# Spectral filter products in column halves, with the moving operand read in memory order

## Chip, cores and metric

The kernel runs on one core of one Trainium2 chip. The metric is device microseconds (us) of the whole program, median of three runs. A core has five engines that run side by side, each through its own list of instructions in order: TensorE (PE in the profile; its weight loads are a row of their own, PEld), VectorE (DVE), ScalarE (ACT), GpSimd (POOL) and SyncE (SP), which here issues all DMAs. Engines wait for each other through semaphores. Matmul results land in PSUM, from where VectorE or ScalarE copy them to SBUF.

## What is computed

Two layers, each with a convolution block done in the frequency domain and a small quantised feed-forward block, on x of shape 8 x 128 x 128 x 96. What matters here is the filter of the convolution block. For each of three scales a coarse complex filter `cw` (rows h, columns w, 192 channels, real and imaginary part) is resized with two cubic matrices, one over rows and one over columns, to 128 x 65 frequencies:

```python
SCALE_HW = [(16, 9), (8, 4), (24, 13)]
x_pre = _soa(jnp.einsum('bhwc,mc->bhwm', x, w1), soa1_scale, soa1_bias)
xf = jnp.fft.rfft2(x_pre.transpose(0, 3, 1, 2), axes=(2, 3), norm='ortho').transpose(0, 2, 3, 1)
for cw in (cw0, cw1, cw2):
    Rh = _resize_mat(cw.shape[0], FH)
    Rw = _resize_mat(cw.shape[1], FWH)
    t = jnp.einsum('Hh,hwmc->Hwmc', Rh, cw)
    t = jnp.einsum('Ww,Hwmc->HWmc', Rw, t)
comb = jnp.einsum('shwm,bsm->bhwm', filt, r.astype(filt.dtype))
xff = xf * comb
```

`r` is a softmax per image over the three scales. The resize over w does not depend on the image, so it is done once for each layer; the one over h, with the image's `r` in it, is done for every image.

## The kernel before

**Stages.** Each image of each layer (16 jobs) is cut into 16 groups. Stage P (`pixels`) normalises 8 rows of pixels, multiplies by w1, and does the first Fourier transform; it ends in DRAM (`a_d`). Stage F (`frequencies`) takes 4 of the 65 columns of frequencies at a time: it loads P's result (`al`) and the filter rows (`ut`), multiplies `ut` by the image's gate on GpSimd (L712), resizes over h on TensorE (`pf`, L724), transforms (`py`), multiplies, and transforms back (`pz`, `pi`). Stage S (`tokens`) ends the inverse transform and does the feed-forward block.

**Order.** The stages run beside each other, one group of each per iteration. The order of all engines' work in an iteration is written out by hand in lists of (stage, step, how many groups ahead): RAMP while only P runs (t from -5 to 14), RISE while P and F run (t from 15 to 34), TICK for the long steady state, then FALL and TAIL. Every engine gets its instructions in this order.

**The filters.** "U" entries in RAMP and RISE are `filters` (L288 to L316), a generator of four steps: the matmuls over w, the ScalarE copies, the VectorE copies, the store to DRAM (`u_d`, read again as `ut` by every F group). A unit covers 8 of the 96 rows (48 coarse rows, real and imaginary) for all 192 channels. There are 12 units for each layer: layer 0's are in RAMP at t = 3 to 14, layer 1's in RISE at t = 21 to 32. The filter is kept as `cw`, 26 partitions (the coarse columns of the three scales) in each of four bands of 32 partitions, one band for 48 channels, with [channel, row] along the partition. A unit is four matmuls, 26 rows deep, 65 columns of weights (`k_rw`), and 384 moving columns (8 rows x 48 channels), one from each band. Their moving operand is read with rows outermost, so neighbouring elements are 96 words apart:

```python
pss[i].rearrange("p (n m) -> p n m", m=UM),
kt["rw"][32 * i : 32 * i + NWS],
cws[l][32 * i : 32 * i + NWS, :, n0 : n0 + UN].rearrange("p m n -> p n m"),
```

The four products lie in four PSUM banks: two of the pair `ps_u` (tag d0) and `ps_v0`, `ps_v1` (tags s3, s4). Two ScalarE copies (L308) and two VectorE copies (L310) of 65 x 384 take them to SBUF, and one DMA (L315) stores 65 x 8 x 192.

**PSUM tags.** A tile waits until the last reader of the tile before it with the same tag is done. In RAMP, d0 is shared by `pa0` (the first transform's product, read by L621 and L622) and `ps_u`; d1 by `pa1` and `pt_a`; d2 by `pw0` and `pw1`; s3 by `ps_v0` and the set-up matmuls' `ps_w`.

**A ramp iteration.** TensorE: U, `pt_a` (L567), `pw` (L578), `pa` twice (L605), `pw`. VectorE: two `at` (L621, L622) of the group before, statistics `st` (L492), the U copies, two `sd` (L596), the norm's small ones ending in `n_rs` (L526), one `sd` (L596), two `at`. GpSimd: two `acc` (L590), `xn_a` (L563, as soon as `n_rs` is there), one `sd`. The `sd` tiles have two buffers, so the last VectorE `sd` of an iteration also waits until the first `pa` has read the older one.

**Set-up.** `background` (L430 to L451) holds the loading of filters and weights in small portions. The main loop takes one portion each iteration, after step 9 of stage P (L1056 to L1058), from t = 0 on. Layer 0's four `cw` loads (L286) are one portion, at t = 0.

Of the kernel before, what the change touches and what calls it, by code (L numbers as in the profile page):

```python
# [11 lines left out]
F32 = mybir.dt.float32  # L12
# [9 lines left out]
M = 2 * C  # L22
# [15 lines left out]
NKC = NKW // KC  # L38
PACK = NKC // 2
GK = 68  # L40
UM = 48
UN = 8
NU = NG // UN
NA, NY = 3, 3
LAG = 3
UAHEAD, UPAUSE, UEND = 3, 18, 35
# [72 lines left out]


RAMP_BANKS = {
    "pa0": 0, "pa1": 1, "pw0": 2, "pw1": 2, "pt_a": 1, "ps_u": 0, "ps_v0": 3, "ps_v1": 4,
}
BANKS = {
    "ps_g": 4, "ph": 3, "pl": 4, "pa0": 1, "pa1": 0, "pw0": 0, "pw1": 0, "pt_a": 0,
# [4 lines left out]
RISE_BANKS = {  # L130
    "ps_g": 3, "ph": 3, "pl": 3, "pa0": 2, "pa1": 0, "pw0": 0, "pw1": 2, "pt_a": 2,
    "pf0": 0, "pf1": 2, "py0": 1, "py1": 1, "pz0": 3, "pz1": 4, "pi0": 3, "pi1": 4,
    "px": 3, "pg": 3, "ps_u": 0, "ps_v0": 3, "ps_v1": 4,
}
FALL_BANKS = {
    "pf0": 0, "pf1": 2, "py0": 1, "py1": 1, "pz0": 3, "pz1": 4, "pi0": 3, "pi1": 4,
# [32 lines left out]
def _constants():  # L169

    n = np.arange(128)
    ang = 2 * np.pi * ((n[:, None] * n[None, :]) % 128) / 128
    cos, sin = np.cos(ang), np.sin(ang)

    even, odd = np.arange(0, 65, 2), np.arange(1, 64, 2)
    bins = ((1, even), (-1, even[1:-1]), (1, odd), (-1, odd))


    f_w = np.concatenate([cos[:64, b] if c > 0 else -sin[:64, b] for c, b in bins], 1) / 128
    f_w = np.concatenate([f_w, f_w], 0)  # L180


    fwd, inv = [], []
    for p in range(2):
        c, s = cos[:HH, p::2], sin[:HH, p::2]
        fwd.append(np.block([[c, -s], [s, c]]))
        inv.append(np.block([[c.T, s.T], [-s.T, c.T]]))

    fwd0, inv0 = np.zeros((2, HH, 2, 2, 2, HH // 2)), np.zeros((2, 2, HH // 2, 2, 2, HH))
    for p in range(2):  # L190
        c, s = cos[:HH, p:HH:2].copy(), -sin[:HH, p:HH:2]
        two = np.full((1, HH // 2), 2.0)
        if p == 0:
            s[:, 0] = cos[:HH, HH]
            two[0, 0] = 1.0
        for b in range(2):
            fwd0[b, :, p, 0, b], fwd0[b, :, p, 1, b] = c, s
            inv0[0, b, :, p, b], inv0[1, b, :, p, b] = (c * two).T, (s * two).T
    fwd0, inv0 = fwd0.reshape(128, 2, 128), inv0.reshape(128, 2, 128)

    d = np.concatenate([cos[b] if c > 0 else -sin[b] for c, b in bins], 0) * 2 / 128
    d[0] /= 2
    d[32] /= 2
    d = d[:, :HH]
    rh = np.concatenate([_resize_mat(h, H) for h, _ in SCALES], 1).T
    rh0 = np.zeros((GP, 2, 2, HH // 2))
    for p in range(2):
        f = np.arange(p, HH, 2)
        rh0[:NHS, 0, p] = (rh[:, f] + rh[:, -f % 128]) / 2
        rh0[64:, 1, p] = (rh[:, f] - rh[:, -f % 128]) / 2  # L210
    rh0[:NHS, 1, 0, 0] = rh[:, HH]
    rh = np.concatenate([rh[:, 0::2], rh[:, 1::2]], 1)
    rh2 = np.zeros((GP, 128))
    rh2[:NHS] = rh
    rh2[64:] = rh
    rw = np.concatenate([_resize_mat(w, NKW) for _, w in SCALES], 1).T
    rw = np.concatenate([rw[:, odd], rw[:, even]], 1)
    rw4 = np.zeros((128, NKW))
    for i in range(M // UM):
        rw4[32 * i : 32 * i + NWS] = rw  # L220
    made = dict(
        dft=f_w, fwd=np.stack(fwd, 1), inv=np.stack(inv, 1), idft=d, rh=rh2, rw=rw4,
        fwd0=fwd0, inv0=inv0, rh0=rh0.reshape(GP, 128),
    )
    return {k: np.ascontiguousarray(v, dtype=np.float32) for k, v in made.items()}
# [15 lines left out]
def metaformer_kernel(ctx: ExitStack, tc: tile.TileContext, x, cst, layers, out):  # L241
# [30 lines left out]
    nc.vector.memset(ones, 1.0)  # L272

    mid = [dram.tile([W, H, C], F32, name=f"mid{b}") for b in range(B)]
    u_d = [dram.tile([NKW, GP, M], F32, name=f"u_d{l}") for l in range(len(layers))]
    a_d = [dram.tile([128, HH, 2, M], F32, name=f"a_d{i}") for i in range(NA)]
    y_d = [dram.tile([128, HH, 2, C], F32, name=f"y_d{i}") for i in range(NY)]


    def load_filters(l, p):  # L280

        cws[l] = us.tile([128, UM, NG], F32, name="cw")
        for i in range(M // UM):
            if l and i:
                yield
            nc.sync.dma_start(cws[l][32 * i : 32 * i + NWS], p["cw"][:, i * UM : (i + 1) * UM, :])  # L286

    def filters(i):  # L288

        l, n0 = i // NU, i % NU * UN  # L290
        pu = bank2("ps_u")
        pss = [pu[:NKW, i, : UN * UM] for i in range(2)]
        pss += [bank1(f"ps_v{i}")[:NKW, : UN * UM] for i in range(2)]
        for i in range(M // UM):
            mm(
                pss[i].rearrange("p (n m) -> p n m", m=UM),
                kt["rw"][32 * i : 32 * i + NWS],
                cws[l][32 * i : 32 * i + NWS, :, n0 : n0 + UN].rearrange("p m n -> p n m"),
                start=True,
                stop=True,  # L300
            )
        yield
        u = us.tile([NKW, UN, M], F32, name="u", bufs=3)
        uv = u.rearrange("p n (i m) -> p i n m", m=UM)
        for i, ps in enumerate(pss):
            o = ps.rearrange("p (n m) -> p n m", m=UM)
            if i < 2:
                nc.scalar.copy(uv[:, i], o)  # L308
            else:
                nc.vector.tensor_copy(uv[:, i], o)  # L310
            if i == 1:
                yield
        yield
        n1 = n0 if n0 < NHS else 64 + n0 - NHS
        nc.sync.dma_start(u_d[l][:, n1 : n1 + UN, :], u)  # L315
        yield  # L316

    def padding(l):
# [110 lines left out]

    def background():  # L430

        yield from load_filters(0, layers[0])
        constants("rw")
        yield
        yield from other_weights(0, layers[0])
        for k in ("fwd", "rh"), ("inv", "rh0"), ("fwd0", "inv0"), ("idft",):
            constants(*k)
            yield
        padding(0)
        yield  # L440
        cw1 = load_filters(1, layers[1])
        for k, _ in enumerate(token_weights(0, layers[0])):
            if k >= 3:
                next(cw1)
            yield
        for _ in cw1:
            yield
        yield
        yield from projection_weights(1, layers[1])
        for _ in zip_longest(other_weights(1, layers[1]), token_weights(1, layers[1])):  # L450
            yield  # L451
# [244 lines left out]
    def frequencies(jb, k):  # L696
# [7 lines left out]
        for p, first in enumerate((re, im)):  # L704
            for e in range(2):
                nc.sync.dma_start(al[64 * p : 64 * p + 64, e], av[:, e, first : first + KC])
        ud = u_d[jb.l].rearrange("k n m -> n k m")
        nc.sync.dma_start(ut[:, 1:], ud[:, k0 : k0 + KC])
        if packed:
            nc.sync.dma_start(ut[:, :1], ud[:, NKW - 1 :])  # L710
# [304 lines left out]
    with tc.manual_schedule():  # L1015
        advance("P", 0, 0)
        start = projection_weights(0, layers[0])
        for _ in range(4):
            next(start)
        events = background()  # L1020
        for t in range(-first, n + offset["S"] + behind + 1):
            norms.append(Norms())
            if t < offset["F"] - 4:
                order, places, late_steps = RAMP, RAMP_BANKS, {}
            elif t < offset["S"] - 2:
                order, places, late_steps = RISE, RISE_BANKS, RISE_GATE
                on_pool.update(sd=())
            elif t < n + 2:
                order, places, late_steps = TICK, BANKS, GATE
            elif t <= n + offset["F"]:  # L1030
                order, places, late_steps = FALL, FALL_BANKS, {}
            else:
                order, places, late_steps = TAIL, TAIL_BANKS, {}
                on_act.update(norm=NORM_ACT_TAIL, cast=CAST_ACT_TAIL, out=False)
            banks.update(places)
            if t == UEND:
                padding(1)
                early.close()
                pools.append(ctx.enter_context(tc.tile_pool(name="sb", bufs=2)))
            gates = {}  # L1040
            for late, into in late_steps.items():
                if (t - late) % NRG == NRG - 1 and 0 <= t - late < n:
                    for place, step in into:
                        gates.setdefault(place, []).append((step, (t - late) // NRG))
            for place, (stage, step, ahead) in enumerate(order):
                for gate_step, image in gates.get(place, ()):
                    advance("G", gate_step, image)
                i = t - offset[stage] + ahead
                last = i if stage == "N" else group(i) if stage == "U" else min(i, n - 1)
                advance(stage, step, last)  # L1050
                if (stage, step, i) == ("N", 0, 1):
                    for late in 1, 2:
                        advance("N", late, i)
                    for _ in start:
                        pass
                if (stage, step) == EVENTS_AFTER:  # L1056
                    if t >= 0:
                        next(events, None)  # L1058


# [38 lines left out]
```

## Time and profile before

| | us |
|---|---|
| median of 3 runs (4893.21 to 4893.49) | 4893.36 |
| the profiled execution's own time | 4890.47 |
| its span in the trace | 4888.7 |

The trace's mean TensorE clock is 0.989 of full. The page gives busy times of engines, a strip of 40 slices of the span, the chain of work that ended last (followed back from the end, at each step to what released it), and the costliest groups of instructions with the mean duration of one. The trace behind the page also answers for a stretch of time: instructions in order, waits, busy times. Times in it are us from the start of the span; a row with "x8" is eight instructions merged. A float32 matmul shows as two records. The ramp runs to 137 us, the fill (first frequencies of the first image) from there to about 174 us, RISE to about 440 us.

### The profile page before, as it was taken

How to read it: one execution, taken by the hardware profiler on the slowest of the kernel's cores; microseconds unless marked ns; L12 is line 12 of the kernel's file. 1: busy time of each engine (PE TensorE's matmuls, PEld its weight loads, DVE VectorE, ACT ScalarE, POOL GpSimd, SP SyncE). 2: the span in 40 equal slices, each digit the busy share in tenths (PEclk: the TensorE clock that was granted, in tenths of full speed). 3: DMA queues.
4: the chain of work that ended last, by engine and by line, in shares of the span. 5: the costliest groups of instructions: out<-in, count | busy, mean ns of one | idle time of the engine just before them, and what ended most of it. 6: DMA issues, size and time to landing. Idle time of an engine off the chain costs nothing.

```text
span 4888.7 us, 123746 instructions
## 1 busy us (share of the span) xinstructions
PE 4799.7 (98%) x44232; PEld 3744.3 (77%) x44232; DVE 4593.7 (94%) x13942; ACT 4311.6 (88%) x7103; POOL 2530.5 (52%) x1884
## 2 busy tenths in 40 slices
PE   8999999999999999999999999999999999999997
PEld 5677777777777777777777778777777777777764
DVE  8888999999999999999999999999999999998998
ACT  7556999999999999999999999999999999998887
POOL 4444555555555555555555555555555555554544
PEclk9999999999999999999999999999999999999996
DMA  6767777777777777777777777777777777777754
GB/s 203 203 192 202 213 213 217 214 213 214 214 214 213 215 214 214 215 212 221 212 214 217 209 216 214 216 215 214 213 214 215 215 214 213 215 215 196 208 168 125
DMA packets 917424, 1020.96 MB, mean 209 GB/s; under 512 B 75826, under 2 KB 848914, under 8 KB 916602
## 3 DMA queue, kind: packets, MB, share of 16 engines
q1 hardware_dynamic: 916810, 1013.04, 74.7%
q8 instruction: 353, 5.78, 0.5%
q14 instruction: 261, 2.14, 0.1%
HBM read 598.92 MB, written 413.84 MB: 207 GB/s over the span
## 4 chain that ended last, share of the span: by engine, by line
PE 90%; DVE 5%; ACT 3%; issue 1%; SPq 0%; POOL 0%; DMA 0%; POOLq 0%; DVEq 0%; ACTq 0%
PE pw L578 17%; PE py L758 14%; PE pz L848 9%; PE pa L605 7%; PE pf L724 7%; PE pi L864 7%; PE pm L943 6%; PE pz L840 5%; PE po L960 5%; PE pt_a L567 5%; PE ps_r L898 4%; PE pt_c L933 2%; DVE st L492 1%; ACT y L946 1%; DVE xr L909 1%
## 5 line engine op out<-in xcount | busy, mean ns | idle before, releaser
L801 POOL TENSOR_TENSOR xf<-pr 128x768 f32<-128x768 f32 x512 | 931.2, 1819 | 416.4 <-DVE pr L786 391.3
L578 PE MATMUL pw<-w,xT 97*128 97x240 f32 x4096 | 942.6, 373 | 6.4 <-DVE at L622 2.9
L758 PE MATMUL py<-k_fwd,al 128*128 128x128 f32 (+1 forms) x6208 | 799.2, 280 | 0.0
L946 ACT CAST y<-pm 128x1024 f16<-128x1024 f32 x768 | 754.8, 1017 | 42.8 <-PE pm L943 42.6
L578 PEld LDWEIGHTS pw<-w,xT 97*128 97x128 f32 x4096 | 741.6, 191 | 59.7 <-ACT r L581 10.9
L953 ACT ACTIVATE h<-a 128x1024 fp8e5<-128x1024 f16 x731 | 775.4, 1061 | 0.2 <-DVE a L949 0.2
L590 POOL TENSOR_TENSOR acc<-acc,r 128x192 f32<-128x192 f32 x496 | 295.8, 596 | 924.1 <-ACT r L581 859.0
L758 PEld LDWEIGHTS py<-k_fwd,al 128*128 128x128 f32 (+1 forms) x6208 | 741.9, 190 | 40.9 <-DVE pr L786 3.3
L978 POOL TENSOR_TENSOR y<-xr,o 128x768 f32<-128x768 f32 x256 | 422.0, 1648 | 677.1 <-DVE o L975 600.9
L581 ACT ACTIVATE r<-pw 128x960 f32<-128x960 f32 x512 | 496.9, 970 | 127.0 <-PE pw L578 125.9
L782 DVE TENSOR_TENSOR pr<-py,cf 128x768 f32<-128x768 f32 x512 | 486.4, 950 | 49.7 <-PE py L758 36.4
L596 DVE TENSOR_TENSOR sd<-xs 128x384 f32<-128x384 f32 x1008 | 521.2, 557 | 1.5 <-ACT xs L584 0.8
L712 POOL TENSOR_TENSOR ut<-ut,rw 112x768 f32<-112x768 f32 (+1 forms) x256 | 473.2, 1848 | 39.0 <-DMA ut<-u_d 34.0
L724 PEld LDWEIGHTS pf<-k_rh,ut 48*128 48x128 f32 x6080 | 360.4, 188 | 151.7 <-issue 140.8
L943 PE MATMUL pm<-xq,f_q 96*128 96x512 fp8e5 x1536 | 431.3, 390 | 27.9 <-ACT y L946 22.0
L563 POOL TENSOR_TENSOR xn_a<-xt,n_rs 128x768 f32<-128x768 f32 x256 | 381.5, 1490 | 128.2 <-DVE n_rs L526 113.1
L936 ACT ACTIVATE xq<-pt_c 96x1024 fp8e5<-96x1024 f32 x256 | 260.8, 1019 | 201.7 <-PE pt_c L933 201.7
L584 ACT ACTIVATE xs<-r 128x768 f32<-128x768 f32 x512 | 436.6, 853 | 0.4
L724 PE MATMUL pf<-k_rh,ut 48*128 48x128 f32 x6080 | 410.1, 281 | 7.5 <-POOL ut L712 3.5
L919 ACT ACTIVATE xn_c<-xr,n_nb,n_rs 128x96 fp8e5<-128x96 f32 x1056 | 412.5, 489 | 0.0
L864 PE MATMUL pi<-zt,k_inv 128*128 128x384 f32 (+1 forms) x1024 | 394.1, 505 | 2.3 <-ACT zt L855 2.2
L848 PE MATMUL pz<-w2c,xf 128*128 128x96 f32 x2048 | 396.0, 275 | 0.0
(133 smaller groups left out, 10124.3 us busy)
## 6 DMA issues: line engine op xcount, KB each, us to landing
a_d<-at SPq DMA_DIRECT2D x256, 768.0 KB
al<-a_d SPq DMA_DIRECT2D x1024, 192.0 KB
y_d<-yt SPq DMA_DIRECT2D x512, 192.0 KB
v<-y_d SPq DMA_DIRECT2D x256, 384.0 KB
ut<-u_d SPq DMA_DIRECT2D x256, 336.0 KB
xt<-in_x_dram SPq DMA_DIRECT2D x512, 96.0 KB
xr<-in_x_dram SPq DMA_DIRECT2D x256, 192.0 KB
mid<-y SPq DMA_DIRECT2D x256, 192.0 KB
```

Source lines behind the costliest of these rows:

```text
L578: mm(o, xT[:, 4 * a + 2 * i + j, :], wt["w1"], start=True, stop=True)
L581: nc.scalar.activation(r.rearrange("p a s c -> p a (s c)"), pw, AF.Relu)
L596: on.tensor_tensor(sd[:, e], xs[:, 0], xs[:, 1], op)
L724: mm(pf[:, i, t * 128 : (t + 1) * 128], utf[64 * i : 64 * i + NHS, c0 : c0 + 128], kt["rh"][64 * i : 64 * i + NHS, :], start=True, stop=True,)
L758: mm(py[p0:p1, t, e, :], alf[:, e, c0 + p0 : c0 + p1], f, start=True, stop=True)
L782: nc.vector.tensor_tensor(p0, yv, crb, ALU.mult)
L801: nc.gpsimd.tensor_tensor(xf.rearrange("p t e f -> p (t e) f"), pr[:, 0].rearrange("p t r k -> p t (r k)"), pr[:, 1].rearrange("p t r k -> ...
L848: mm(pz[t][:, j, e, :], xf[:, 2 * t, e, :], wt["w2c" if t else "w2a"], start=False, stop=j == e == 1,)
L864: mm(pi[e][:, lo : KC * C], kt["inv"][:, e, :], zt[:, e, lo:], start=True, stop=True)
L943: mm(pm[:, s, :], fk, xq[:, s, :], start=True, stop=True)
L946: nc.scalar.copy(y16, pm)
L953: nc.scalar.activation(hk, a16, AF.Copy, saturate=False)
```

## The change

Filter products have 64 columns of weights instead of 65; `cw` lies in two bands of 32 partitions with 96 channels each; a unit covers 4 coarse rows of the real and the same 4 of the imaginary part. The four matmuls of a unit are two bands times two halves of the PSUM partitions (0 to 63 real, 64 to 127 imaginary). The moving operand is read in memory order, 4 neighbouring rows of a channel, then the next channel. One ScalarE and one VectorE copy of 128 x 384, reading PSUM with a step of 4 elements, turn it to [row, channel]. Two DMAs store a unit. The 65th frequency, whose weights only pick the last column of each scale, comes from six small loads, two transposes, one ScalarE copy and two stores for each layer. `ps_u` is gone. Portions of `background` are smaller and more, and begin at t = -3. The rows of `u_d` are padded from 112 to 128.

```diff
-UM = 48
-UN = 8
-NU = NG // UN
+UN = 4
+HC = C // 2
+NU = NHS // UN
...
-    "pa0": 0, "pa1": 1, "pw0": 2, "pw1": 2, "pt_a": 1, "ps_u": 0, "ps_v0": 3, "ps_v1": 4,
+    "pa0": 0, "pa1": 1, "pw0": 2, "pw1": 2, "pt_a": 1, "ps_v0": 3, "ps_v1": 4,
...
-    rw4 = np.zeros((128, NKW))
-    for i in range(M // UM):
-        rw4[32 * i : 32 * i + NWS] = rw
+    rw2 = np.zeros((64, 64))
+    for h in range(2):
+        rw2[32 * h : 32 * h + NWS] = rw[:, :-1]
...
-    u_d = [dram.tile([NKW, GP, M], F32, name=f"u_d{l}") for l in range(len(layers))]
+    u_d = [dram.tile([NKW, 128, M], F32, name=f"u_d{l}") for l in range(len(layers))]
...
     def load_filters(l, p):
 
-        cws[l] = us.tile([128, UM, NG], F32, name="cw")
-        for i in range(M // UM):
-            if l and i:
+        cws[l] = us.tile([64, C, NG], F32, name="cw")
+        for h in range(2):
+            for n in range(0, C, HC):
+                nc.sync.dma_start(
+                    cws[l][32 * h : 32 * h + NWS, n : n + HC],
+                    p["cw"][:, C * h + n : C * h + n + HC, :],
+                )
                 yield
-            nc.sync.dma_start(cws[l][32 * i : 32 * i + NWS], p["cw"][:, i * UM : (i + 1) * UM, :])
+        last = us.tile([C, 2, NG], F32, name="cw_last")
+        h0 = w0 = 0
+        for h, w in SCALES:
+            w0 += w
+            to = last.rearrange("p u (r n) -> p u r n", r=2)[:, :, :, h0 : h0 + h]
+            end = p["cw"][w0 - 1].rearrange("(u p) (r n) -> p u r n", u=2, r=2)
+            for u in range(2):
+                nc.sync.dma_start(to[:, u], end[:, u, :, h0 : h0 + h])
+            h0 += h
+        yield
+        ps = bank1("ps_w")[:NG, :M]
+        for u in range(2):
+            nc.tensor.transpose(ps[:, u * C : (u + 1) * C], last[:, u], ident[:C, :C])
+        ends = us.tile([NG, M], F32, name="cw_end")
+        nc.scalar.copy(ends, ps)
+        yield
+        for r in range(2):
+            nc.sync.dma_start(u_d[l][NKW - 1, 64 * r : 64 * r + NHS, :], ends[NHS * r : NHS * r + NHS])
 
     def filters(i):
 
         l, n0 = i // NU, i % NU * UN
-        pu = bank2("ps_u")
-        pss = [pu[:NKW, i, : UN * UM] for i in range(2)]
-        pss += [bank1(f"ps_v{i}")[:NKW, : UN * UM] for i in range(2)]
-        for i in range(M // UM):
-            mm(
-                pss[i].rearrange("p (n m) -> p n m", m=UM),
-                kt["rw"][32 * i : 32 * i + NWS],
-                cws[l][32 * i : 32 * i + NWS, :, n0 : n0 + UN].rearrange("p m n -> p n m"),
-                start=True,
-                stop=True,
+        pss = [bank1(f"ps_v{h}")[:, : UN * C] for h in range(2)]
+        for h, ps in enumerate(pss):
+            q = slice(32 * h, 32 * h + NWS)
+            for i in range(2):
+                n1 = NHS * i + n0
+                mm(
+                    ps[64 * i : 64 * i + 64].rearrange("p (m n) -> p m n", m=C),
+                    kt["rw"][q],
+                    cws[l][q, :, n1 : n1 + UN],
+                    start=True,
+                    stop=True,
+                )
+        yield
+        u = us.tile([128, UN, 2, C], F32, name="u", bufs=3)
+        nc.scalar.copy(u[:, :, 0], pss[0].rearrange("p (m n) -> p n m", m=C))
+        yield
+        nc.vector.tensor_copy(u[:, :, 1], pss[1].rearrange("p (m n) -> p n m", m=C))
+        yield
+        for i in range(2):
+            nc.sync.dma_start(
+                u_d[l][:64, 64 * i + n0 : 64 * i + n0 + UN, :].rearrange("k n m -> k (n m)"),
+                u[64 * i : 64 * i + 64].rearrange("p n h m -> p (n h m)"),
             )
...
     def background():
 
+        constants("rw")
         yield from load_filters(0, layers[0])
-        constants("rw")
-        yield
         yield from other_weights(0, layers[0])
...
         for k, _ in enumerate(token_weights(0, layers[0])):
-            if k >= 3:
+            if k >= 1:
                 next(cw1)
             yield
-        for _ in cw1:
-            yield
-        yield
+        yield from cw1
...
-        ud = u_d[jb.l].rearrange("k n m -> n k m")
+        ud = u_d[jb.l].rearrange("k n m -> n k m")[:GP]
...
                 if (stage, step) == EVENTS_AFTER:
-                    if t >= 0:
+                    if t >= -3:
                         next(events, None)
```

## Prediction, made before the changed kernel was run

> **What bounds the kernel now.** I read the page's totals first, then the answer for the filter's tile, then the chain of waits in the ramp and in RISE, then the instructions in order of time where VectorE and GpSimd meet. Totals:
>
> ```profile
> span 4888.7 us, 123746 instructions
> PE 4799.7 (98%) x44232; PEld 3744.3 (77%) x44232; DVE 4593.7 (94%) x13942; ACT 4311.6 (88%) x7103; POOL 2530.5 (52%) x1884
> PE 90%; DVE 5%; ACT 3%; issue 1%; SPq 0%; POOL 0%; DMA 0%; POOLq 0%; DVEq 0%; ACTq 0%
> ```
>
> TensorE carries the whole, but VectorE is close behind, and the change only touches the ramp and RISE (the steady state's lists of instructions stay as they are). The answer for the tile ps_u:
>
> ```profile
> L295 PE MATMUL ps_u<-cw,k_rw x96: 804/816/836, 48.0 to 387.3; 26*65 26x384 f32 x96
> L308 ACT COPY u<-ps_u x48: 474/476/478, 49.6 to 388.5; 65x384 f32<-65x384 f32 x48
> ```
>
> A record of a filter product takes 816 ns (the middle figure). The first transform pa (L605), also 384 columns, takes 482 ns a record in the same stretch: the stepped read costs about twice. What a unit costs on the path is in the chain (start, us, what), here one ramp iteration:
>
> ```profile
> 100.22 0.77 PE ps_u L295 x2
> 100.99 0.01 PE ps_v L295 x2
> 101.00 0.63 PE ps_u L295 x2
> 101.63 0.01 PE ps_v L295 x2
> 101.65 1.01 PE pt_a L567 x8
> 102.65 1.62 PE pw L578 x8
> 104.28 1.45 PE pa L605 x16
> 105.73 1.82 PE pw L578 x8
> 107.55 0.77 PE ps_u L295 x2
> ```
>
> The iteration is 107.55 - 100.22 = 7.33 us, TensorE without a gap; the unit is 0.77 + 0.01 + 0.63 + 0.01, with starts 1.43 apart. Four products run at once (the ps_v rows add 0.01). In RISE the chain shows the same 1.43 (272.91 to 274.34) within iterations of about 16 us, again all TensorE. So the unit lies on the path in all 24 of its places.
>
> One thing could spoil this. In the ramp VectorE is busy 76.92 of 81.5 us (48.03 to 129.53). Its last sd of an iteration behaves in two ways. First an iteration before the units begin, then one with them:
>
> ```profile
> 37.48 0.17 DVE L526 SCALAR_TENSOR_TENSOR n_rs<-n_a,n_rs 128x8 f32<-128x8 f32 x1
> 37.73 1.47 POOL L563 TENSOR_TENSOR xn_a<-xt,n_rs 128x768 f32<-128x768 f32 x1 [2.21 <-DVE n_rs L526]
> 37.74 1.88 DVE L596 TENSOR_TENSOR sd<-xs 128x384 f32<-128x384 f32 x1
> ```
>
> ```profile
> 97.72 0.17 DVE L526 SCALAR_TENSOR_TENSOR n_rs<-n_a,n_rs 128x8 f32<-128x8 f32 x1
> 97.89 0.56 DVE L596 TENSOR_TENSOR sd<-xs 128x384 f32<-128x384 f32 x1
> 97.96 1.82 POOL L563 TENSOR_TENSOR xn_a<-xt,n_rs 128x768 f32<-128x768 f32 x1 [3.27 <-DVE n_rs L526]
> ```
>
> Whichever of sd and xn_a starts first runs through; if it is xn_a, sd takes 1.88 instead of 0.56, and in those iterations TensorE's pt_a stands 1.56 us for L622 (at 41.62). sd is late when it still waits for the first pa (at 45.23: "0.30 <-PE pa L605").
>
> [...]
>
> **The change, part by part.**
>
> *Products.* As many matmuls as before (96) with 384 columns each. pa is the nearest row: eight matmuls, four at a time, in 1.45, so four in 0.725. I take a unit at 0.73, saving 0.70. Bounds: 0.6 [...] and 0.9 [...]; serial halves are a rival below.
>
> *Copies.* Half as many: 24 fewer on ScalarE (476 ns), 24 fewer on VectorE (544 ns, starts 0.47 apart). They read PSUM with a step of 16 bytes, which no row of before shows element by element. [...] Bounds: 0.54, as now, and 0.95, half rate; I take 0.54[...].
>
> *Ramp, 12 units.* TensorE's iteration becomes 7.33 - 0.70 = 6.63. VectorE from sd to sd (97.89 to 105.22) has 0.2 idle for n_rs from ScalarE (97.12 to 97.31) and 0.09 before L621 (98.45 to 98.54); less one copy: 7.33 - 0.29 - 0.47 = 6.57, plus a little of that waiting. ScalarE's u, xs, xT, n_rs come earlier with the shorter unit, so n_rs is not late. The two engines end almost level; I take 6.65, 0.68 less each time: 12 x 0.68 = 8.2. Off this: 0.24 at the first unit, whose next pt_a cannot start before L622 at 48.31 + 0.54 + 0.14 = 48.99 (it started at 49.45 to 49.52); 0.6 for set-up memsets on VectorE (0.54 and twice 0.12), which had cover in its 0.29 of idle and have none now; 0.4 for an sd that loses to xn_a now and then. Without ps_u the tag d0 no longer makes the unit wait for L622 (0.46 at 48.03 and the stretch up to 78.16), but pt_a waits for the next L622 anyway. Ramp: -7.0. Does sd win? With VectorE the later engine it starts at once after n_rs, 0.07 before xn_a, so yes; where TensorE is ahead, the margin is a few hundredths.
>
> *Start.* The four cw loads (1.79 of SP issue at 22.22, 468 KB each) move between the pixel loads of the iterations t = -3 to 0; k_rw too. The third group's pixels come about 0.9 later in issue and then queue behind 468 KB, 2 to 3 us at the 150 to 190 GB/s of that stretch. VectorE idles 2.44 after that group's norm (20.76 to 23.19, waiting for n_rs), which hides about 1.4 of late landing. At t = 1 six small loads (at 0.3 to 0.7 of SP each, 2 to 4 us) go where SP had about 1.5 spare and pixels are loaded five groups ahead; SP has a second store per unit (0.33). The two transposes (0.38 for a like pair, L683) come at t = 2, where TensorE stands 1.56; cw_end's ScalarE copy (0.35) also has slack there, behind the slow sd. The transposes wait for the six loads, issued an iteration (7.5) earlier; behind them on TensorE stand pw and both pa, so a late landing would move the whole ramp. The stores of cw_end wait on SP for that copy, with pixel loads behind them that have iterations to spare. I take +0.4; between 0 and +3.
>
> *Fill, 137 to 174 us.* The portions after the filter's move on by two iterations. So the six casts of L425 to L427 (145.67 to 146.66, in the chain between ssum and hm, 0.92) leave the gate's chain for a place where VectorE has room (28.35 busy of 33.37). L656 can come up to 0.92 sooner; TensorE's clock is low in part there, so I count -0.6. The two b_f loads (1.47 of SP) come just before the first al, but SP stands from 145.56 to 149.13 for a_d's landing: hidden; without that, +1.5.
>
> *RISE, 12 units.* VectorE is busy 151.2 of 179.5 us and ScalarE 103.6, so TensorE stays the bound: 12 x 0.70 = 8.4 less 0.4 for layer 1's transposes. xn_a is ready at 272.62, before the unit starts at 272.84, so pt_a can follow sooner. Six loads delay one al by up to 4 us, with an iteration to spare. RISE: -8.0. Afterwards order and sizes are as before, and the lead stays; the padded rows of u_d give ut a step of 98,304 bytes, the one with which al reads a_d already: nothing.
>
> Sum: -7.0 + 0.4 - 0.6 - 8.0 = -15.2. Against its own time of 4890.47 the profiled execution becomes 4875.3; the median shown is 2.9 higher than it, so 4893.4 - 15.2 = 4878.2.
>
> **Rivals.**
>
> *A, copies and reads dearer.* VectorE copy 0.95: its loop is 6.57 + 0.41, about 7.05, the ramp gains 12 x 0.28 - 1.2 = 2.2; unit 0.9: RISE gains 12 x 0.53 - 0.4 = 6.0. With +0.4 - 0.6: -8.4, 4885. For it: no row shows such a PSUM read.[...]
>
> *B, sd loses every time.* If TensorE leads, sd waits for pa and xn_a passes it. VectorE's loop is then 6.57 + 1.32 = 7.9, the ramp loses 12 x 0.57 = 6.8, RISE still gains 8.0: -1.4, 4892. For it: the iterations without units do this. Against: then VectorE is late, pt_a waits for it, and one u copy (0.47) more than covers the 0.30 by which sd was early.
>
> *C, slower: the column halves don't run beside each other.* Four products in line, 4 x 0.73 = 2.9, are 1.5 more than now, 24 times: +36, 4929. It decides from a unit of 1.43 on. For it: no 32 x 64 tile in the trace. Against: pa overlaps in both directions.
>
> That the products stay at stepped speed (the change doing nothing for the read) is A at its worst, 1.43 again and only copies saved: about 4893.
>
> **Numbers.** Forecast 0.72 (of it 0.04 under the bound below), A 0.13 (0.03 over it), B 0.08, C 0.07. A measurement of this kernel can tell about 0.2%, 9.8 us, from no change: faster means under 4883.6. Faster 0.68 + 0.03 = 0.71; slower 0.07; same 0.22. The likeliest case's own range, from the bounds of unit, start and fill, is 4871 to 4884. The range that holds 8 in 10 goes from 4870 (unit 0.6, all 0.92 of the fill, no start cost, ramp at 6.6, and a little unforeseen) to 4889, which takes in A and leaves out most of B and C.
>
> **What would show it.** Filter records near 480 ns and about 0.73 from unit to pt_a in the chain; iterations near 6.65 in the ramp and 0.7 shorter in RISE; a VectorE u copy near 0.54; sd at 0.56 with xn_a behind it; casts gone from between ssum and hm. I am wrong if filter records stay near 800, if they stand one after another, if sd shows 1.9 in the ramp, or if the first unit starts later than 48.

## The result and the profile after

| | before | after |
|---|---|---|
| median, us (executions) | 4894.40 (22) | 4884.58 (22) |
| lowest to highest | 4889.29 to 4903.68 | 4878.51 to 4892.03 |
| profiled execution's own time | 4890.47 | 4892.03 |
| its span | 4888.7 | 4890.1 |

The changed kernel is faster by 9.8 us: the ratio is 0.9980, with a 95% interval of 0.9974 to 0.9986. The forecast was 15.2 less, 4878.2. The one profiled execution of the changed kernel is the slowest of its 22, that of the kernel before lies 4 us under its median; so the two spans show no gain, and the comparison has to go stage by stage.

In the changed kernel everything behind `filters` stands 16 lines lower: `xn_a` is L579, `pt_a` L583, `pw` L594, `sd` L612, `pa` L621, `at` L637 and L638, `ut` L728; the products are L317, their copies L326 (ScalarE) and L328 (VectorE). From the page after, the same totals as before and the row of the DMA queue (packets, MB, share of the 16 engines):

```profile
span 4890.1 us, 123756 instructions
PE 4800.1 (98%) x44236; PEld 3756.7 (77%) x44236; DVE 4585.0 (94%) x13918; ACT 4305.3 (88%) x7081; POOL 2529.9 (52%) x1884
...
q1 hardware_dynamic: 921466, 1013.17, 79.5%
...
PE 90%; DVE 4%; ACT 4%; issue 1%; DMA 1%; SPq 0%; POOL 0%; POOLq 0%; DVEq 0%; ACTq 0%
```

The reader is to see two things: TensorE still carries the chain, and DMA, at 0% of it before, is now at 1%. The queue's row of before read

```profile
q1 hardware_dynamic: 916810, 1013.04, 74.7%
```

The same bytes keep the DMA engines busy for 4.8 points more of the span. Nothing in the prediction speaks of this.

The filter's products and copies after, from the answer for the tile ps_v:

```profile
L317 PE MATMUL ps_v<-cw,k_rw x192: 481/506/532, 50.8 to 377.6; 26*64 26x384 f32 x192
L326 ACT COPY u<-ps_v x24: 473/478/481, 51.8 to 378.2; 128x384 f32<-128x384 f32 x24
L328 DVE COPY u<-ps_v x24: 531/544/557, 53.0 to 380.4; 128x384 f32<-128x384 f32 x24
```

A record falls from 816 to 506 ns; the copies, now with a step of 16 bytes in PSUM, cost what they cost without one. The ramp in the chain of waits after, two iterations:

```profile
57.93 0.80 PE ps_v L317 x8
58.73 1.01 PE pt_a L583 x8
59.74 1.62 PE pw L594 x8
61.36 1.45 PE pa L621 x16
62.81 1.83 PE pw L594 x8
...
64.73 0.98 ACT r L597
...
66.10 1.05 PE pt_a L583 x8
67.15 1.62 PE pw L594 x8
68.77 1.45 PE pa L621 x16
70.22 1.82 PE pw L594 x8
72.04 0.80 PE ps_v L317 x8
```

The unit is 0.80 where 1.43 stood. But the two iterations take 72.04 - 57.93 = 14.11, a mean of 7.05, not 6.65, and in the second one TensorE isn't the last: ScalarE's `r` and `u` stand in the chain. The reason is in the order of time on VectorE and GpSimd:

```profile
55.59 0.17 DVE L542 SCALAR_TENSOR_TENSOR n_rs<-n_a,n_rs 128x8 f32<-128x8 f32 x1
...
55.68 0.55 DVE L612 TENSOR_TENSOR sd<-xs 128x384 f32<-128x384 f32 x1
55.84 1.72 POOL L579 TENSOR_TENSOR xn_a<-xt,n_rs 128x768 f32<-128x768 f32 x1 [3.19 <-DVE n_rs L542]
...
61.87 0.17 DVE L542 SCALAR_TENSOR_TENSOR n_rs<-n_a,n_rs 128x8 f32<-128x8 f32 x1
...
62.11 1.47 POOL L579 TENSOR_TENSOR xn_a<-xt,n_rs 128x768 f32<-128x768 f32 x1 [2.37 <-DVE n_rs L542]
62.30 1.69 DVE L612 TENSOR_TENSOR sd<-xs 128x384 f32<-128x384 f32 x1 [0.27 <-PE pa L621]
```

The first `sd` starts ahead of `xn_a` and takes 0.55; the next one stands 0.27 for `pa`, `xn_a` passes it, and it takes 1.69. After that VectorE is late. TensorE has to wait for it, and in the next iteration `pa` is done before VectorE comes to its `sd`, which therefore starts at once and wins. From 83.22 on wins and losses alternate; in all, `sd` loses in five of the twelve iterations with a unit.

Where the time went, by stage. Each group of pixels starts with an `xn_a` on GpSimd; the table takes its start in each trace, less that in the kernel before (negative: earlier), and shows how much this lead changes from stage to stage. Groups 5, 18, 21, 34 and 40 mark the stages; the last column is from group 255 to the end of the span. All numbers are us, worked out from the order of time on GpSimd; from the fourth row on they are those of the next section.

| trace | start | ramp | fill | RISE | 34 to 40 | steady | end |
|---|---|---|---|---|---|---|---|
| predicted | +0.4 | -7.0 | -0.6 | -8.0 | 0 | 0 | 0 |
| after | +3.09 | -4.83 | +1.51 | -9.47 | +4.34 | +1.05 | +5.71 |
| again | +0.03 | -4.82 | -0.29 | -9.35 | +5.97 | +1.19 | +5.57 |
| rows112 | +0.16 | -4.79 | -1.23 | -9.21 | +1.51 | +0.65 | +5.91 |
| sd3 | +2.14 | -8.59 | -0.59 | -8.89 | -0.06 | +1.08 | +7.71 |
| sd3_rows112 | +1.74 | -8.59 | -1.08 | -8.99 | +4.34 | +0.85 | +2.43 |
| sd3_112_fill2 | +2.11 | -8.54 | -1.84 | -8.70 | +0.41 | +0.21 | +5.55 |
| stepped | +3.21 | -0.23 | -0.13 | -1.99 | +4.32 | +0.65 | +5.67 |
| aligned | +0.24 | -4.81 | -0.68 | -9.15 | -0.14 | +0.64 | +2.60 |
| sd3_aligned | -0.73 | -8.68 | -1.55 | -8.87 | +2.69 | +0.78 | +4.36 |
| best | -0.71 | -8.33 | -0.49 | -8.58 | +0.40 | -0.14 | +0.95 |
| before_sd3 | +2.14 | -1.32 | -3.00 | +0.30 | -0.01 | +0.16 | -0.47 |
| before128 | -0.49 | -0.01 | -1.27 | +0.03 | +6.12 | -0.02 | +5.14 |
| before_off32 | +3.23 | 0.00 | +1.01 | 0.00 | +4.46 | +0.71 | +7.79 |

For one kind of products and of `sd` buffers the ramp and RISE repeat to a few tenths from trace to trace. The start, groups 34 to 40 and the end do not, and kernels that keep the old products lose there too.

The traces show what goes with the losses at the start and in groups 34 to 40: stretches in which TensorE runs slow in that execution. A record of `pw` takes 607 ns at first and 366 later. This changes at 22 to 24 us in seven of the fourteen traces and at 31 to 32 us in the other seven, and these are the seven with +1.7 to +3.2 at the start. For groups 34 to 40 it is the clock that TensorE was granted. From 440 to 460 us the views of before and again read (the last three columns are the granted clock, the DMA share and GB/s):

```profile
440.00:460.00 20.00, 18.94 (x160) 14.02 (x158) 18.29 (x51) 10.57 (x20) 10.29 (x9) 1.00 0.77 226
440.00:460.00 20.00, 18.18 (x117) 14.01 (x117) 15.13 (x46) 8.55 (x17) 8.04 (x6) 0.76 0.77 202
```

Eight traces have a granted clock of 0.5 for 3.4 to 13.7 us between 380 and 480 us. They lose 1.5 to 6.1 in groups 34 to 40, 0.39 to 0.45 us for each us at 0.5. The other six have no such stretch and lose 0.4 at most. Both kinds of products are among the eight.

### The profile page after: what moved, and what is told of

Its sections match the earlier page's. It is cut to its first block, busy times and chain, and to the rows that moved or that the text cites. A ratio compares the mean times of both kernels' runs of the same rounds, so it can differ in the third digit from the quotient of the medians.

```text
span 4890.1 us, 123756 instructions
## 1 busy us (share of the span) xinstructions
PE 4800.1 (98%) x44236; PEld 3756.7 (77%) x44236; DVE 4585.0 (94%) x13918; ACT 4305.3 (88%) x7081; POOL 2529.9 (52%) x1884
## 3 DMA queue, kind: packets, MB, share of 16 engines
q1 hardware_dynamic: 921466, 1013.17, 79.5%
## 4 chain that ended last, share of the span: by engine, by line
PE 90%; DVE 4%; ACT 4%; issue 1%; DMA 1%; SPq 0%; POOL 0%; POOLq 0%; DVEq 0%; ACTq 0%
PE pw L594 17%; PE py L774 14%; PE pz L864 9%; PE pf L740 7%; PE pa L621 7%; PE pi L880 7%; PE pm L959 6%; PE pz L856 5%; PE po L976 5%; PE pt_a L583 5%; PE ps_r L914 4%; PE pt_c L949 2%; ACT y L962 1%; DVE st L508 1%; ACT xn_c L935 1%
## 5 line engine op out<-in xcount | busy, mean ns | idle before, releaser
L594 PE MATMUL pw<-w,xT 97*128 97x240 f32 x4096 | 946.1, 374 | 5.8 <-DVE at L638 3.5
L594 PEld LDWEIGHTS pw<-w,xT 97*128 97x128 f32 x4096 | 744.4, 192 | 57.8 <-ACT r L597 10.7
L612 DVE TENSOR_TENSOR sd<-xs 128x384 f32<-128x384 f32 x1008 | 525.0, 560 | 3.2 <-PE pa L621 3.1
L728 POOL TENSOR_TENSOR ut<-ut,rw 112x768 f32<-112x768 f32 (+1 forms) x256 | 472.3, 1845 | 55.1 <-DMA ut<-u_d 35.1
L579 POOL TENSOR_TENSOR xn_a<-xt,n_rs 128x768 f32<-128x768 f32 x256 | 379.5, 1482 | 118.5 <-DVE n_rs L542 100.0
L781 ACT COPY cf<-pf 128x768 f32<-128x768 f32 x496 | 372.7, 801 | 26.8 <-PE pf L740 26.4
```

Of the source, the lines that this page charges most:

```text
L594: mm(o, xT[:, 4 * a + 2 * i + j, :], wt["w1"], start=True, stop=True)
L612: on.tensor_tensor(sd[:, e], xs[:, 0], xs[:, 1], op)
L728: nc.gpsimd.tensor_tensor(ut[:, -n:], ut[:, -n:], _bc_mid(jb.rw, n), ALU.mult)
```

## The experiments

Medians of all runs, each beside the kernel before on the same chip (its median lay from 4894.15 to 4895.35 there):

| run | median us (executions) | ratio to before, 95% interval | DMA share |
|---|---|---|---|
| again | 4886.35 (10) | 0.9983, 0.9974 to 0.9992 | 79.4% |
| sd3 | 4879.69 (6) | 0.9966, 0.9954 to 0.9979 | 79.3% |
| before_sd3 | 4892.59 (13) | 0.9994, 0.9986 to 1.0003 | 74.9% |
| stepped | 4898.92 (13) | 1.0007, 0.9999 to 1.0015 | 79.3% |
| rows112 | 4883.81 (12) | 0.9976, 0.9968 to 0.9984 | 79.0% |
| before128 | 4894.64 (13) | 0.9999, 0.9991 to 1.0008 | 74.2% |
| sd3_rows112 | 4880.54 (6) | 0.9972, 0.9960 to 0.9983 | 79.2% |
| sd3_112_fill2 | 4878.99 (5) | 0.9965, 0.9952 to 0.9977 | 79.4% |
| aligned | 4879.19 (6) | 0.9970, 0.9959 to 0.9982 | 74.8% |
| before_off32 | 4896.79 (13) | 1.0001, 0.9993 to 1.0010 | 79.2% |
| best | 4876.94 (5) | 0.9961, 0.9948 to 0.9973 | 75.0% |
| sd3_aligned | 4877.40 (5) | 0.9964, 0.9950 to 0.9977 | 75.0% |

**again: the same kernel, a second trace.** No edit.

> The changed kernel once more, for a second trace. If the late start (first xn_a groups about 3 us behind the kernel before), the loss in the fill (about 2.7 us) and the stall of 5.65 us behind mid at 4454 belong to the kernel, they stand here again within 0.5 us. If they belong to that one execution, they are gone and the profiled span is 5 to 10 us shorter than 4890. The pairs of about 14.05 us in the ramp should be there in either case, and the records of the filter products at about 506 ns.

The loss of 3 us at the start is gone (+0.03), the loss in the fill too (-0.29), and the span is 3 us shorter. Pairs of about 14 us in the ramp, 506 ns a record and a stall behind `mid` near 4450 stand again. The other two losses, in groups 34 to 40 and at the end, remain. So the start and the fill of the first trace belong to that execution; `before_sd3` and `before_off32` show the same +2 to +3 at the start with the old loads. In those traces TensorE's matmuls stay slow about 8 us longer. From the chain of after:

```profile
25.84 3.57 PE pw L594 x8
29.40 1.71 PE pt_a L583 x8
```

and of before:

```profile
25.55 1.90 PE pw L578 x8
...
34.12 1.05 PE pt_a L567 x8
```

**sd3 and before_sd3: does the lost `sd` cost the ramp?** In the changed kernel, and in the kernel before alike:

```diff
-            sd = ab.tile([128, 2, 2, M], F32, name="sd")
+            sd = ab.tile([128, 2, 2, M], F32, name="sd", bufs=3)
```

> The changed kernel with a third buffer for sd, so that the second sd of an iteration no longer waits 0.27 us for pa. Theory [...]: sd then always starts before xn_a and takes 0.55 us everywhere in the ramp; the iterations there fall from a mean of 7.02 to about 6.65 us, and the kernel gets about 12 x 0.37 = 4.4 us faster, with another 2 to 3 from the iterations without units (sd 1.88 there): 4 to 7 us below the changed kernel, ratio to it about 0.9988. Rival (TensorE or ScalarE sets the ramp anyway): sd is shorter, the iterations stay at 7.0, and the time stays within 1 us.

> The kernel before with a third buffer for sd and nothing else. Theory [...]: its iterations with units keep 7.33 us, since sd already wins there and TensorE has no gap; only the four or so iterations ahead of the units, where sd takes 1.88, get about 0.5 to 1 us shorter each: 2 to 3 us in all, ratio 0.9995. If the gain here is as large as in the changed kernel (4 us or more), the buffer helps both alike, and the change didn't bring the loss that is put down to it.

With the third buffer VectorE's `sd` takes 0.55 in the iterations with units and never more than 0.77 (1.70 in the changed kernel), and there the chain in sd3 is TensorE without a gap:

```profile
56.34 0.80 PE ps_v L317 x8
57.14 1.01 PE pt_a L583 x8
58.15 1.62 PE pw L594 x8
...
61.22 1.82 PE pw L594 x8
63.04 0.80 PE ps_v L317 x8
```

An iteration is 63.04 - 56.34 = 6.70. The ramp gains 8.59 rather than 4.83, and the median falls by 4.9 to 4879.69. In the kernel before the same edit gives 1.3 in the ramp, 0.9 of it ahead of the units. The median is 2.6 lower, as forecast, but the ratio's interval takes in no change. Its iterations with units keep 7.33, but for one, in which `sd` had lost in the kernel before as well:

```profile
75.27 1.76 DVE L596 TENSOR_TENSOR sd<-xs 128x384 f32<-128x384 f32 x1 [0.20 <-PE pa L605]
```

That iteration takes 8.16 in before and 7.52 in before_sd3. So `sd` loses in one of twelve iterations with units before the change and in five of twelve after it, and most of the loss came with the change: at 6.7 the two engines are nearly level, and which of them is the later changes from one iteration to the next.

**stepped: order of the read, or halves?** The changed kernel with the old order:

```diff
-                    ps[64 * i : 64 * i + 64].rearrange("p (m n) -> p m n", m=C),
+                    ps[64 * i : 64 * i + 64].rearrange("p (n m) -> p n m", m=C),
...
-                    cws[l][q, :, n1 : n1 + UN],
+                    cws[l][q, :, n1 : n1 + UN].rearrange("p m n -> p n m"),
...
-        nc.scalar.copy(u[:, :, 0], pss[0].rearrange("p (m n) -> p n m", m=C))
+        nc.scalar.copy(u[:, :, 0], pss[0].rearrange("p (n m) -> p n m", m=C))
```

and VectorE's copy likewise.

> The changed kernel, with the halves, the stores and the 65th frequency as they are, but the moving operand read as before (channels innermost, a step of 94 floats from one to the next) and PSUM in that order, so that the copies need no step. Theory (the order of the read is what pays): records of the filter products go back to about 816 ns, the unit to 1.43, the ramp iteration to about 7.35 and RISE to 16.0: the gain of both stages, 15 us, goes, and what remains are 24 copies and the new loads: 4893 to 4896. Rival (64 columns and 48 fewer copies pay too): records of 600 to 700 ns and half of the gain stays, 4887 to 4890. ScalarE's and VectorE's copies of u stay at 478 and 544 ns if a step of 16 bytes in PSUM costs nothing, and fall if it does.

From the answer for the tile ps_v in stepped:

```profile
L317 PE MATMUL ps_v<-cw,k_rw x192: 814/824/837, 50.9 to 388.1; 26*64 26x384 f32 x192
L326 ACT COPY u<-ps_v x24: 478/479/482, 52.4 to 389.0; 128x384 f32<-128x384 f32 x24
L328 DVE COPY u<-ps_v x24: 528/551/558, 53.2 to 390.6; 128x384 f32<-128x384 f32 x24
```

The whole read price is back, the unit is 1.43 and the ramp's gain is 0.23: the gain is the order of the read. The copies without a step take 479 and 551 ns, with one 478 and 544: no cost of the step in PSUM shows. `sd` loses in six of the twelve iterations with a unit here too (1.57 to 1.88), but their mean stays at 7.41, where the kernel before has 7.40: with a unit of 1.43 and one VectorE copy fewer than in the kernel before, a lost `sd` costs little.

What is left is 1.99 in RISE. There the first `pw` behind the unit takes 1.62 in the chain of stepped, as in that of aligned; in the kernel before it takes 1.82 in every iteration with a unit. The trace of before names the wait, that of its weight load for the unit's copy:

```profile
275.28 1.51 PEld L578 LDWEIGHTS pw<-w,xT 97*128 97x128 f32 x8 [0.18 <-ACT u L308]
```

It stands in all twelve iterations, 2.2 us in sum, and in none of after, stepped and aligned. The median came out above the forecast, by 2.9 at the least; this kernel carries the new place of the buffers too, which is told below.

**rows112 and before128: is it the step of u_d?** The DMA share had risen, so the first suspect was the new row count:

```diff
-    u_d = [dram.tile([NKW, 128, M], F32, name=f"u_d{l}") for l in range(len(layers))]
+    u_d = [dram.tile([NKW, GP, M], F32, name=f"u_d{l}") for l in range(len(layers))]
```

and the reverse, with `[:GP]` on the read of `ud`, in the kernel before.

> The changed kernel, with u_d at 112 rows for each frequency as in the kernel before (a step of 86,016 bytes from one frequency to the next) in place of 128 (98,304 bytes); nothing else differs. Theory (the step): the DMA share of the queue falls from 79.4% back to about 74.8%, and since every ut transfer is then shorter, the stall of 5.7 us behind mid near 4450 is gone from the chain and the first ut of the fill lands 1 to 2 us sooner: the median 2 to 6 us under the changed kernel's 4885. Rival (the share has another source, such as the halved stores of u or cw_last): the share stays near 79.4%. Third (the step costs DMA time but none on the path): the share falls, the median stays within 1.5 us.

> The kernel before with u_d at 128 rows for each frequency and nothing else. Theory (the step): the DMA share rises from 74.7% to about 79.4% and the time by 2 to 6 us, ratio 1.0004 to 1.0012. Rival (other source): the share stays at 74.7%. Third (no path): the share rises, the time stays within 1.5 us.

The theory fell both ways: rows112 keeps 79.0%, before128 keeps 74.2%, and neither median moves by more than a measurement can tell. That the padded rows cost no time that shows had been forecast rightly.

**aligned and before_off32: is it the place of the buffers?** What else differs for every transfer is the place in SBUF. `k_rw` shrank from 260 to 256 bytes a partition, and in the compiled programs the tiles that the steady transfers use (`xt`, `at`, `al`, `ut`, `yt`, `v`, `xr`, `y`) stand 32 bytes lower, off the multiples of 64 at which they stood. The edit of aligned puts them back:

```diff
-    rw2 = np.zeros((64, 64))
+    rw2 = np.zeros((64, 72))
...
-        rw2[32 * h : 32 * h + NWS] = rw[:, :-1]
+        rw2[32 * h : 32 * h + NWS, :64] = rw[:, :-1]
...
-                    kt["rw"][q],
+                    kt["rw"][q, :64],
```

before_off32 widens `rw4` of the kernel before by eight columns of zeros in the same way.

> The changed kernel with k_rw at 72 columns (8 of zeros that no product reads) in place of 64. k_rw is 260 bytes a partition in the kernel before and 256 in the changed one; [...]every later buffer, the ones that transfers go to and from among them, moved down by 32 bytes (xt from 45,888, a multiple of 64, to 45,856, which is none). Here they are back at multiples of 64. Theory (the place of the buffers): the DMA share falls from 79.4% to about 74.8% though not one transfer differs; if that costs time, the stall behind mid near 4450 is gone and the median is 2 to 5 us lower, 4880 to 4883. Rival (the share comes from the new stores and loads): the share stays at 79.4%. Third (share without time): the share falls and the median stays at 4884 to 4886.

> The kernel before with k_rw at 73 columns (8 of zeros), which moves every later buffer up by 32 bytes, off the multiples of 64. Theory (the place): the DMA share rises from 74.7% to about 79.4%; if that costs time, 2 to 5 us more than the kernel before, ratio 1.0004 to 1.001. Rival: the share stays at 74.7%. Third: the share rises and the time stays within 1.5 us.

The page's row of the queue, in aligned:

```profile
q1 hardware_dynamic: 921466, 1013.18, 74.8%
```

and in before_off32:

```profile
q1 hardware_dynamic: 916810, 1013.04, 79.2%
```

The share follows the place in both directions, with packets and bytes as they were. The traces also tell which packets pay. Those of 768 bytes take a mean of 47.7 and 46.9 ns in before and aligned between 600 and 1000 us, and 52.4 and 52.6 in before_off32 and after. That is 40 to 41% against 45% of the 16 engines' time, most of the difference. Packets of 1536 and 6144 bytes differ by 3% at most.

In time, aligned is 5.4 us under the changed kernel (the intervals of the two ratios overlap a little), while before_off32 is only 1.4 above the kernel before, inside its interval. Part of the 5.4 may be the clock's: the mean granted clock is 0.989 over the six executions of aligned and 0.987 over the 22 of the changed kernel. TensorE hides the dearer packets in the steady state (busy 399.9 of 400 us from 600 to 1000 in both kernels and in these two); what is left to look at are places where transfers are late anyway. The end is one: with its stages running out, the changed kernel's chain has

```profile
4452.31 1.94 ACT y L962 x2
...
4454.33 5.65 DMA xr<-mid
4459.98 0.02 DVEq L887
```

and again has 5.74 at the same wait (4451.27). That one wait isn't the rule: no other trace of either place has it. Over the whole end, from 4430 on, waits for a DMA make up 2.6 to 10.2 us of the chain in the six traces with buffers at multiples of 64 (before, before_sd3, before128, aligned, sd3_aligned, best), a mean of 5.7, and 0 to 24.5, a mean of 11.9, in the eight off them. In the table by stage the first kind loses -0.5 to 5.1 at the end against the kernel before, a mean of 2.5 over five, the second 2.4 to 7.8, a mean of 5.8.

But the granted clock is a rival here. Between 4400 and 4600 us it is 0.5 for up to 17 us of a trace, and the loss at the end goes with that: none in before and before_sd3 (the table's 0 and -0.5), 6.8 us in aligned and best (2.6 and 1.0), 10.2 to 17.1 in the other ten (2.4 to 7.8). Two of these ten, sd3_aligned and before128, have buffers at multiples of 64. Whether late transfers bring the low clock about was not tried. That the place sets the share is shown. That it costs time the medians point to; in the end of a trace it can't be told from the clock, and its size isn't firm.

**sd3_rows112 and sd3_112_fill2: the fill.** In the first trace of after the fill's chain waited for the first `ut`, behind layer 1's `cw` loads:

```profile
149.39 8.78 DMA ut<-u_d
```

The edit starts those loads two iterations later:

```diff
-            if k >= 1:
+            if k >= 3:
```

> The changed kernel with the third buffer for sd and u_d at 112 rows. If both losses are separate and add up: 4879.7 less 2 to 6, so 4874 to 4878, ratio to the kernel before about 0.996; ramp iterations at 6.705 us, DMA share about 74.8%. If the step costs nothing on the path, 4879 to 4880.

> As the run ahead of it, with layer 1's portions of the filter's loads starting two iterations later, so that no cw load of 468 KB is issued in the iteration in which the first ut is. Theory (queueing behind cw in the fill): the first ut lands in about 6 us or less instead of 8.8, and the groups after the fill start 1 to 3 us sooner; the median falls by as much. Rival (ut waits for a_d's and al's own traffic there): the landing stays above 6 us, and the time within 1 us of the run ahead of it. A loss is possible too: the loads then stand just ahead of layer 1's first unit, which would wait for them.

The landing is shorter in this pair of traces: 7.75 in sd3_rows112, and in the chain of sd3_112_fill2

```profile
143.77 6.23 DMA ut<-u_d
```

Group 19 starts 1.1 sooner, but by group 21 only 0.3 of lead is left, and the medians differ by 1.6, within their spread. The wait is in the traces; that moving the loads is worth anything isn't shown. sd3_rows112 beside sd3 shows no effect of the step of u_d either: 79.2 against 79.3%, 4880.54 against 4879.69.

**best and sd3_aligned.** The edits of sd3 and aligned together, in best with that of the fill as well.

> The changed kernel with the third buffer for sd, layer 1's filter loads two iterations later and the buffers back at multiples of 64. If all three add up: 4879 less 2 to 5 for the place, 4874 to 4877, ratio 0.996; DMA share 74.8%, ramp iterations 6.705 us. If the place costs no time: 4878 to 4880.

> The changed kernel with the third buffer for sd and the buffers back at multiples of 64, the loads of layer 1 where the change put them. It tells whether the 5 us of the place (4884.6 to 4879.2, six executions alone) are real and add to the 5 us of the third buffer (4879.7). If they add up: 4874 to 4876, and the later loads in the best version bring nothing more (4876.9). If the gain by place was chance: 4879 to 4880, as with the third buffer alone. If both remove the same stall: 4877 to 4879. DMA share 74.8%, ramp iterations 6.705 us.

4876.94 lies at the upper end of what best was to show if all added up, 4877.40 in the third case of sd3_aligned, in which the two repairs share part of their gain. Aligned buffers are worth 2.3 on top of the third buffer, and 2.1 between sd3_112_fill2 and best, less than the 5.4 of aligned alone. With five or six executions each, neither difference is firm by itself; taken together, the ten executions with both repairs have a median of 4877.4 and the 17 with the third buffer alone 4879.6. With 4876.9 to 4877.4, best and sd3_aligned beat both kernels: 17 to 18 us under the kernel before, 7 under the changed one. Between these two the later loads make no difference that can be told.

## Why the prediction was right, and what it missed

The time, 4884.6, lies inside the range from 4870 to 4889, and it fell, as forecast, because the read got cheaper. But it is 6.4 above the forecast and just outside the likeliest case's own 4871 to 4884: the range held because it was drawn to take in rival A, not because the ramp had been foreseen.

**Products.** Right in kind. The unit was taken at 0.73, from `pa`; that pieces of four floats would be read as fast as `pa`'s operand was the author's estimate, and so were the bounds of 0.6 and 0.9. It is 0.80, inside them, its records 506 ns and not 482. The step at every fourth element may be what is left of the price; the runs don't separate it from the other shape of the tiles. The saving is 0.63 a unit, 24 x 0.07 = 1.7 us less than forecast.

**Copies.** Right: 544 and 478 ns. That 0.54 was likelier than 0.95 had been the author's estimate. The result equals the time of rival A, 4885, but not by A's cause.

**Rival C** fell: the halves stand side by side, four products in 0.80. What the order of the read is worth stands in stepped: 824 against 506 ns a record in the same tiles. Pieces of another length than four floats were not tried.

**Ramp: the mis-sized term.** The sum took off "0.4 for an sd that loses to xn_a now and then". Iterations have a mean of 7.0 rather than 6.65, and 12 x 0.37 = 4.4 is what that term should have been; sd3 gives back 4.9 in the median, of which some 1.3 was there to be had in the kernel before as well. That the ramp fell short by 2.2 and not by 4.0 is because two other terms were off the other way. The sum took every iteration of the kernel before at 7.33, but the one with the lost `sd` at 75.27 took 8.16; and what was charged apart for the first unit and the memsets is in the mean of 7.0. So 8.2 + 0.8 - 4.4 = 4.6, beside 4.8 measured. The argument had put both ends right (where pa is the later, sd waits for it and loses; where VectorE is the later, sd wins) and then taken the second for a stable state. Each state makes the other: a lost `sd` makes VectorE the later one, and then the next `sd` wins. The slow `sd` at 75.27, in an iteration with a unit, was in the trace of before and could have warned. Where two engines end "almost level", half of the iterations is a better guess than now and then. Rival B, at half its strength, was the case.

**Start.** +0.4 was about right: 0.0 to 0.2 in again, rows112 and aligned, three of the seven traces in which a record of `pw` falls from 607 to 366 ns at 22 to 24 us. The +3 of other traces goes with the later 32 us and comes with the old loads as well.

**Fill.** -0.6 against -0.3, -1.2 and -0.7 in again, rows112 and aligned: it fits, but kernels with the old products scatter from -3.0 to +1.0 there, so it isn't confirmed. The low clock that the forecast speaks of is 0.66 from 145 to 155 us in the kernel before. The casts left the chain; the landing of the first `ut` took their place, and wasn't named.

**RISE.** -8.0, measured -9.1 to -9.5. The units give 12 x 0.63 = 7.5, and the shorter `pw` behind each, 0.20 x 12 = 2.4, was not in the sum; it stands in stepped too, so it doesn't come with the order of the read. In the kernel before `ps_u` and `pw0` share the bank tag d0 in RISE, so that `pw` had to wait for the unit's copies: the twelve waits shown with stepped. Taking `ps_u` away by itself was not tried.

**What the sum lacked.** "Afterwards order and sizes are as before, and the lead stays." Order and sizes did stay, but the places of the transfers' buffers moved by 32 bytes, because one constant became 4 bytes shorter. This is a share of DMA time that was nowhere in the reckoning. What it costs is open: the pairs of runs above differ by 2 to 5 us in the changed kernel, and part of that may be the clock's.

With both of these mended, sd3_aligned is 16.8 us under the kernel before on the same chip; less the part of the third buffer that is not the change's (1.3 in the ramp of before_sd3), some 15.4 are left, against 15.2 in the forecast. That the sum closes so well is partly luck: the units brought less than forecast, and the shorter `pw` in RISE and the one slow iteration of the kernel before made up for it.

## What to carry to other kernels

Where a saving brings two engines level, look in the trace for what the instruction that starts second takes (here `sd`: 0.55 us ahead of `xn_a`, 1.69 behind it), and count on the bad order in up to half of the iterations (here five of twelve); a third buffer was the cheap way out (8.59 us gained in the ramp, not 4.83). When a constant or an early buffer changes its size, look at the places of everything allocated behind it (here 32 bytes lower, with 79.5% of DMA time instead of 74.7%). And compare stages at fixed instructions, not spans, and read the granted clock beside each: here single traces of one kernel differ by 3 to 6 us where TensorE ran slow in one and not in the other.

## What was not expected of the hardware

- The transfers' SBUF buffers at multiples of 64 bytes or 32 bytes off them: 74.2% to 75.0% against 79.0% to 79.5% of DMA time for the same bytes, in fourteen traces of both kernels and their variants and without an exception. Packets of 768 bytes take 46.7 to 47.7 ns in the first kind and 51.9 to 52.6 in the second, from 600 to 1000 us. Whether another step than 64 would do as well was not tried.
- A moving operand in pieces of four floats (16 bytes) takes 506 ns for 384 columns; one with a step at every element takes 824, and the transform with long pieces 482.
- Stretches in which TensorE runs slow come and go with the execution and set 3 to 6 us of a trace: at the start (a record of `pw` at 607 ns until 24 or until 32 us, 366 after that), in groups 34 to 40, and in the end, where `pf` took 2.86 at 4485.31 in after and 1.54 at 4487.36 in before, with a granted clock of 0.72 and 1.00 from 4480 to 4492 us. What starts such a stretch stays open.
